# Self edges taken out of the gathers of a relational graph layer: compacted rows of 267 edges

## The chip, the cores and the metric

One core of a Trainium2 chip. The metric is the device time of one execution in microseconds, the median of several runs.

## The reference

A graph layer with a normalisation ahead of it and a residual sum behind it. 12500 nodes of 256 values, 212500 edges, 8 edge types. The edges are sorted by destination with a stable sort; 12500 of them go from a node to itself, and since they were appended last, each node's own edge is the last of its edges.

```python
def ref(edge_index, x, edge_type, weight, h_bias, loop_weight):
    src, dst = edge_index
    hx = einsum('ni,rio->rno', x, weight)            # one product per type
    msg = hx[edge_type, src]
    agg = segment_sum(msg, dst, num_segments=num_nodes)
    node_repr = agg * 0.5 ** 0.5 + h_bias
    return node_repr + (x @ loop_weight) * 0.5 ** 0.5

h = maximum(layernorm(x, axis=-1), 0.0)
return x + ref(stack([src, dst]), h, edge_type_8, weight, h_bias, loop_weight)
```

## The kernel before

The kernel sums first and multiplies afterwards: for every node and every type it adds up the rows of h whose edges arrive there, and only then applies the eight weights. Everything is fp32.

*Tiles and units.* 128 edges make a tile, two tiles a unit (`PAIR`): 1661 tiles, 831 units. The edge indices are loaded as rows of 256 (`load_indices`), one row per unit, 128 rows to a block, seven blocks. `sources` turns the source indices over, so that a column of `gidx` holds the 128 sources of a tile; `columns` works out for each edge a column, 8 times the node's distance from the row's first node plus the type, and `places` the row's offset in the accumulator.

*Edges.* `gather(t)` fetches the 128 rows of a tile from h by an indirect DMA on POOL (L479). `onehots` compares the columns with a constant row on VectorE (L492). `edge_sums` multiplies messages by one-hots on PE into PSUM (L520): 168 columns for a unit's first tile and 136 for its second (`REACH`), each in two chunks of 128 features. `add_sums` adds a unit's 336 columns into the accumulator at an offset held in a register (L532). Each fp32 matmul stands in the profile as two records.

*The accumulator.* `acc` is a ring of six slots (`SLOTS`), each of 128 nodes, features on partitions: `[128, 2, 8, 6 * 128 + 2 * WIN]`. A slot is zeroed on ScalarE by `clear` (L546), six groups ahead.

*Groups.* 98 groups of 128 nodes. When all units that can touch a group are added (`plan.last`), its work is queued: `own` transposes the group's rows of h into a PSUM buffer (tag `pt`, a pool of one buffer that all transposes use), copies them to `self_t`, and adds the bias to x; 18 products (L606: two with the loop weight, sixteen with the type weights) go into `po`; `finish` adds `po` to x, stores four groups at a time, and clears a slot. h and x come back from memory four groups at a time (`load_groups`, on SP's queue).

*The start.* h must exist before it is gathered. The kernel therefore reads all of x in pieces (`load_rows`), normalises on VectorE and ScalarE (`norm_rows`, `moments`) and stores h (`h32`). The first 96 tiles gather rows of x instead and are normalised in place (`batch`); later ones gather h.

*Order.* The order on each engine is written by hand: one loop over tiles, `gather` running 58 tiles ahead (`AHEAD`; 62 message buffers), one-hots 8 to 11 ahead (`LEAD`), `add_sums` one unit behind (`LAG`). Steps of the next block's preparation are put into a `background` list with the tile at which each is due. Group products are spread between edge sums by a budget: each has a cost and a tile by which it must be out (`until`).

```python
until = PAIR * (plan.first[g + SLOTS] - 2) - REST if g + SLOTS < plan.NG else NT - 1
ready = t + max(0, min(DELAY, NT - 1 - t - 2 * DELAY))
...
while queue and (budget > 0 and t >= queue[0][0] or t >= queue[0][1]):
```

*The fallback.* A count of edges that fitted their row's window is compared with the number of edges; if it differs, `general_path` computes everything anew, edge by edge.

Of the kernel before, what the change touches and what calls it, by code (L numbers as in the profile page):

```python
# [20 lines left out]
P = 128  # L21
# [4 lines left out]
XG = 4  # L26


WIN = 21
REACH = ((0, 21), (4, 17))  # L30
# [4 lines left out]
CLEARED = 3  # L35
# [23 lines left out]
PREP = 30  # L59
STEP = 3  # L60

# [3 lines left out]
class Plan:  # L65
# [6 lines left out]
    def __init__(self, N, E):  # L72
        self.NT = -(-E // P)
        self.NU = NU = -(-self.NT // PAIR)
        U = PAIR * P
        slack = 6.5 * (E / 4) ** 0.5 / U + 1.0
        self.rate = rate = E / (N * U)

        self.low = [(1 / rate, -slack / rate), (1.1 / rate, -(1.5 + 0.1 * E / U) / rate)]
        self.high = [(1 / rate, slack / rate)]  # L80
        self.starts = list(range(0, N, GROUP))
        self.ends = self.starts[1:] + [N]
        self.NG = len(self.starts)
        self.last = [
            min([NU - 1, *(int((e + 2 - b) / a) + 1 for a, b in self.low)]) for e in self.ends]
        self.last[-1] = NU - 1
        a, b = self.high[0]
        self.first = [max(0, int((s - WIN - 2 - b) / a) - 1) if s else 0 for s in self.starts]

# [101 lines left out]
def kernel(  # L191
# [20 lines left out]
    NJ = N // P  # L212
    NM = NJ * P
    NR = N - NM

    NT = plan.NT
    NTF = E // P
    EL = E - (NT - 1) * P

    U = PAIR * P  # L220
    NU = plan.NU
    NUF = E // U
    EU = E - NUF * U
    NB = -(-NU // P)
    scale = ALPHA**0.5
# [10 lines left out]
    zero = const.tile([P, 1], F32, name="zero")  # L236
    bias_in = const.tile([P, D], F32, name="bias_in")
    w = const.tile([P, KC, R * D], F32, name="w")
    wl = const.tile([P, KC, D], F32, name="wl")
    gidx = const.tile([P, NB * PAIR * P], I32, name="gidx")  # L240
    col = const.tile([P, NB, PAIR, P], F32, name="col")
    low = const.tile([P, NB], F32, name="low")
    high = const.tile([P, NB], F32, name="high")
    counts = const.tile([P, NB], F32, name="counts")
    flag = const.tile([1, 1], I32, name="flag")
    NK = -(-N // RING)
    wraps = const.tile([P, NK], F32, name="wraps")

    def edges(t):
        return P if t < NTF else EL  # L250
# [6 lines left out]
    with ExitStack() as main:  # L257
# [5 lines left out]
        rowp = main.enter_context(tc.tile_pool(name="rowp", bufs=ROWS))  # L263
        small = main.enter_context(tc.tile_pool(name="small", bufs=4))
        msgs = main.enter_context(tc.tile_pool(name="msgs", bufs=MSGS // PAIR))
        ohs = main.enter_context(tc.tile_pool(name="ohs", bufs=2 + LEAD // QUAD))
        dense = main.enter_context(tc.tile_pool(name="dense", bufs=2))
# [4 lines left out]
        iota_f, bias_bc = fixed[:, :C], fixed[:, C : C + D]  # L272
        assert C + D <= 512
# [3 lines left out]
        added, zeroed = {}, {}  # L277
# [3 lines left out]
        def load_indices(b):  # L281
            nat = {}
            for name, a, pad in (("s", src, 0), ("d", dst, -1), ("t", etype, 0)):
                n = ep.tile([P, U], I32, name=f"nat_{name}")
                full = min(P, NUF - b * P)
                if full < P:
                    nc.vector.memset(n, pad)
                e0 = b * P * U
                if full:
                    nc.sync.dma_start(  # L290
                        n[:full, :], a[e0 : e0 + full * U].rearrange("(p q) -> p q", q=U))
                if full < P and EU:
                    nc.sync.dma_start(
                        n[full : full + 1, :EU], a[NUF * U : E].rearrange("(p q) -> p q", p=1))
                nat[name] = n
            return nat

        def turned(got, cols, to):

            def turn():  # L300
                pt = ps_d.tile([P, D], F32, tag="pt", name="ptr")
# [3 lines left out]
                nc.vector.tensor_copy(to, pt[:, : PAIR * P])  # L305

            return [turn]

        def sources(b, got):
            def copy():  # L310
                got["sf"] = ep.tile([P, U], F32, tag="part", name="sf")
                nc.vector.tensor_copy(got["sf"], got["s"])

            return [copy] + turned(got, "sf", gidx[:, b * PAIR * P : (b + 1) * PAIR * P])

        def columns(b, got):
# [4 lines left out]
            def bases():  # L321
                got["base"] = small.tile([P, PAIR], F32, name="base")
                nc.vector.tensor_scalar(
                    got["base"][:, 0:1], got["d"][:, 0:1], low[:, b : b + 1], high[:, b : b + 1],
                    op0=ALU.max, op1=ALU.min)

            def second():
                nc.vector.tensor_scalar(
                    got["base"][:, 1:2], got["base"][:, 0:1], float(REACH[1][0]), None, op0=ALU.add)

            def relative():
                got["rel"] = ep.tile([P, U], F32, name="rel")
                for i, (h, _, _) in enumerate(halves):
                    nc.vector.tensor_scalar(
                        got["rel"][:, h], got["d"][:, h], got["base"][:, i : i + 1], None,
                        op0=ALU.subtract)

            def from_():
                got["ok"] = ep.tile([P, U], F32, tag="part", name="ok")
                nc.vector.tensor_scalar(got["ok"], got["rel"], 0.0, None, op0=ALU.is_ge)  # L340

            def to():
                for h, _, n in halves:
                    nc.vector.scalar_tensor_tensor(
                        got["ok"][:, h], got["rel"][:, h], float(n), got["ok"][:, h],
                        op0=ALU.is_lt, op1=ALU.mult)

            def typed():
                nc.vector.scalar_tensor_tensor(
                    got["rel"], got["rel"], float(R), got["t"], op0=ALU.mult, op1=ALU.add)  # L350

            def final():
                nc.vector.scalar_tensor_tensor(
                    got["rel"], got["rel"], 1.0, got["ok"], op0=ALU.add, op1=ALU.mult)
                nc.vector.tensor_reduce(counts[:, b : b + 1], got["ok"], AX.X, ALU.add)

            return [bases, second, relative, from_, to, typed, final] + turned(
                got, "rel", col[:, b, :, :].rearrange("p i u -> p (i u)"))

        def places(b, got):  # L360
# [16 lines left out]
            def turn():  # L377
                pt = ps_d.tile([P, D], F32, tag="pt", name="ptr")
# [6 lines left out]
        def verdict(got):  # L385
# [5 lines left out]
            def compare():  # L391
                pt = ps_d.tile([P, D], F32, tag="pt", name="ptr")
# [10 lines left out]
        def prepare(b):  # L403
# [3 lines left out]
                lambda: got.update(load_indices(b)), *sources(b, got), *columns(b, got),  # L407
                *places(b, got), *(verdict(got) if b == NB - 1 else [])]


        x_main = x[:NM].rearrange("(p j) d -> p j d", p=P)
        h_main = h32[:NM].rearrange("(p j) d -> p j d", p=P)
        groups = [(j, min(XG, NJ - j), P) for j in range(0, NJ, XG)]
        if NR:
            groups.insert(1, (NJ, 1, NR))

# [24 lines left out]
        def load_rows(i):  # L441
            if i < len(groups):
                j0, nj, n = groups[i]
                xts[i] = rowp.tile([P, XG, D], F32, tag="rows", name="xt")
                if n == P:
                    nc.sync.dma_start(xts[i][:, :nj, :], x_main[:, j0 : j0 + nj, :])
                else:
                    nc.sync.dma_start(xts[i][:n, 0, :], x[NM:])

        def norm_rows(i):  # L450
            j0, nj, n = groups[i]
            xt = xts.pop(i)
            after = moments([xt[:n, j, :] for j in range(nj)], n, nj, "n_")

            def rest():
                after()
                if n == P:
                    nc.sync.dma_start(h_main[:, j0 : j0 + nj, :], xt[:, :nj, :])
                else:
                    nc.sync.dma_start(h32[NM:], xt[:n, 0, :])  # L460
# [5 lines left out]
        def gather(t):  # L466
            n = edges(t)
# [6 lines left out]
            else:  # L474
# [3 lines left out]
            at = (b * PAIR + i) * P + u  # L478
            nc.gpsimd.indirect_dma_start(  # L479
                out=msg[t][:n], out_offset=None, in_=table[:, :],  # L480
                in_offset=bass.IndirectOffsetOnAxis(ap=gidx[:n, at : at + 1], axis=0))

        def onehots(t):
# [5 lines left out]
            for v, i in ((n // PAIR, PAIR), (1, n % PAIR)):  # L489
                if v and i:  # L490
                    cols = col[:, b, :i, u + k : u + k + v].rearrange("p i u -> p u i")
# [3 lines left out]
                        cols.unsqueeze(3).to_broadcast([P, v, i, C]), op=ALU.is_equal)  # L495
# [13 lines left out]
        def edge_sums(t):  # L509
            n = edges(t)  # L510
# [8 lines left out]
            for c in range(KC):  # L519
                nc.tensor.matmul(  # L520
                    ps[:, c, from_ : from_ + width], m[:n, c * P : (c + 1) * P], o[:n, :width],
# [6 lines left out]
        def add_sums(u, ps):  # L528
# [5 lines left out]
            for g in range(1, plan.NG):  # L534
                if plan.first[g] == u:
                    assert not plan.first[g] or (g, "slot") in zeroed
                    for k in [k for k in zeroed if k[0] == g or k[1] == "wrap"]:
                        tc.add_manual_dep(
                            i.ins, zeroed.pop(k).name, SYNC_DEP, reason="columns are empty")


        def clear(g):

            s0 = plan.starts[g] % RING
            a = acc[:, :, :, s0 : s0 + GROUP].rearrange("p c r d -> p (c r) d")
            i = nc.scalar.activation(a, zero.unsqueeze(2).to_broadcast([P, KC * R, GROUP]), AF.Copy)  # L546
            zeroed[g, "slot"] = i.ins
# [3 lines left out]
        def load_groups(q):  # L551

            d0, d1 = plan.starts[XG * q], plan.ends[min(plan.NG, XG * (q + 1)) - 1]
            full, rest = divmod(d1 - d0, P)
            for name, table in (("h", h32), ("x", x)):
                rows_ = got[name, q] = rowp.tile([P, XG, D], F32, tag="rows", name=f"{name}r")
                if full:
                    nc.sync.dma_start(
                        rows_[:, :full, :],
# [270 lines left out]
```

## Time and profile before

| | |
|---|---|
| median of 3 runs | 2112.68 us (2111.18 to 2114.15) |
| profiled execution | 2568.97 us, its span 2567.2 us |
| PE busy in the profile | 2019.2 us (79%), 10405 records |
| VectorE | 920.8 us (36%) |
| ScalarE | 342.8 us (13%) |
| POOL | 1572.7 us (61%) |
| granted TensorE clock, mean | 0.891 |
| gathers L479 | 1661, 946 ns each |
| edge sums L520 | 6644 records |
| products L606 | 3528 records |

The profiled execution is one execution with the profiler on, and its time is its own; the median is of executions without it. A row of a group ends with the busy time, the mean of one instruction in ns, and the idle time ahead of it with what ended it. "issue" is idle time for which the profile shows no cause. A timeline row starts with start and length in us. Ends of matmuls are modelled.

### The profile page before, as it was taken

How to read it: one execution, taken by the hardware profiler on the slowest of the kernel's cores; microseconds unless marked ns; L12 is line 12 of the kernel's file. 1: busy time of each engine (PE TensorE's matmuls, PEld its weight loads, DVE VectorE, ACT ScalarE, POOL GpSimd, SP SyncE). 2: the span in 40 equal slices, each digit the busy share in tenths (PEclk: the TensorE clock that was granted, in tenths of full speed). 3: DMA queues.
4: the chain of work that ended last, by engine and by line, in shares of the span. 5: the costliest groups of instructions: out<-in, count | busy, mean ns of one | idle time of the engine just before them, and what ended most of it. 6: DMA issues, size and time to landing. Idle time of an engine off the chain costs nothing.

```text
span 2567.2 us, 28487 instructions
## 1 busy us (share of the span) xinstructions
PE 2019.2 (79%) x10405; PEld 1736.7 (68%) x10405; DVE 920.8 (36%) x2101; ACT 342.8 (13%) x446; POOL 1572.7 (61%) x1686
## 2 busy tenths in 40 slices
PE   1148888888888788888888888888888888878789
PEld 1137767677777677677767676777667676667678
DVE  3476333333333333333333333333333333343333
ACT  3574101010100101011010100101001010101010
POOL 7435666666666666666666666666666666666640
PEclk9558899898898989889888999999898889999999
DMA  5682433333433333343333343333333333333320
GB/s 185 202 294 85 119 88 115 115 91 115 120 90 115 102 102 116 91 119 113 92 114 116 90 121 115 88 115 101 108 115 92 114 115 91 115 114 92 114 82 13
DMA packets 131293, 288.61 MB, mean 112 GB/s; under 512 B 29032, under 2 KB 71878, under 8 KB 131152
## 3 DMA queue, kind: packets, MB, share of 16 engines
q0 software_dynamic: 79712, 217.71, 29.2%
q1 hardware_dynamic: 51440, 69.05, 8.2%
q8 instruction: 85, 1.39, 0.2%
q14 instruction: 56, 0.46, 0.1%
HBM read 261.04 MB, written 25.60 MB: 112 GB/s over the span
## 4 chain that ended last, share of the span: by engine, by line
PE 75%; issue 17%; DVE 3%; another core or an unknown queue 2%; ACT 1%; DMA 1%; POOL 0%; SPq 0%; DVEq 0%; ACTq 0%; POOLq 0%
PE ps L520 40%; PE po L606 34%; PE pst L573 1%; DVE e_stats L422 1%; DMA h<-xt 1%; ACT xt L434 0%; DMA w<-in_L_gnn_weight_dram 0%; DVE n_stats L422 0%; ACT msg L434 0%; DVE n_mv L424 0%; DVE acc L532 0%; POOL msg L479 0%; DVE e_mv L424 0%; DVE oh L492 0%
## 5 line engine op out<-in xcount | busy, mean ns | idle before, releaser
L479 POOL DMA_INDIRECT msg<-h,gidx x1565 | 1480.2, 946 | 829.7 <-issue 417.0
L520 PE MATMUL ps<-oh,msg 128*128 128x168 f32 x6644 | 1301.7, 317 | 376.2 <-issue 230.1
L520 PEld LDWEIGHTS ps<-oh,msg 128*128 128x128 f32 x6644 | 1157.5, 208 | 563.3 <-issue 344.4
L606 PE MATMUL po<-w,acc 128*128 128x256 f32 x3136 | 1008.4, 410 | 114.0 <-issue 106.9
L606 PEld LDWEIGHTS po<-w,acc 128*128 128x128 f32 x3136 | 563.8, 206 | 181.4 <-issue 164.6
L532 DVE TENSOR_TENSOR acc<-acc,ps 128x336 f32 x831 | 413.7, 498 | 679.5 <-PE ps L520 350.9
L492 DVE TENSOR_TENSOR oh<-fixed,col 128x672 f32<-128x672 f32 x416 | 354.5, 852 | 770.9 <-remote 360.6
L546 ACT ACTIVATE acc<-zero 128x2048 f32<-128x2048 f32 x98 | 187.2, 1912 | 682.8 <-PE ps L520 374.5
L575 ACT ACTIVATE self_t<-pst 128x256 f32<-128x256 f32 x98 | 37.4, 382 | 1397.5 <-remote 650.4
L479 POOL DMA_INDIRECT msg<-in_x_dram,gidx x96 | 91.0, 947 | 82.9 <-issue 58.9
L606 PE MATMUL po<-wl,self_t 128*128 128x256 f32 x392 | 120.0, 418 | 24.6 <-issue 20.3
L606 PEld LDWEIGHTS po<-wl,self_t 128*128 128x128 f32 x392 | 73.1, 206 | 46.5 <-issue 38.4
L434 ACT ACTIVATE xt<-xt,n_shift,n_rstd 128x256 f32<-128x256 f32 (+1 forms) x98 | 50.9, 588 | 21.5 <-DVE n_shift L431 7.3
L434 ACT ACTIVATE msg<-msg,e_shift,e_rstd 128x256 f32<-128x256 f32 x96 | 49.8, 589 | 24.9 <-DVE e_shift L431 10.3
L573 PE MATMUL pst<-ident,hr 128*128 128x128 f32 x196 | 40.2, 285 | 15.9 <-issue 13.9
L615 DVE TENSOR_TENSOR xr<-xr,po 128x256 f32<-128x256 f32 x98 | 40.4, 413 | 10.7 <-PE po L606 7.8
L573 PEld LDWEIGHTS pst<-ident,hr 128*128 128x128 f32 x196 | 28.6, 149 | 20.4 <-issue 16.2
L576 DVE TENSOR_TENSOR xr<-xr,fixed 128x256 f32<-128x256 f32 x98 | 40.5, 413 | 3.6 <-issue 3.6
L422 DVE BATCH_NORM_STATS2 n_stats<-xt 128x6 f32<-128x256 f32 (+1 forms) x98 | 34.4, 412 | 0.8 <-issue 0.8
L422 DVE BATCH_NORM_STATS2 e_stats<-msg 128x6 f32<-128x256 f32 x96 | 33.5, 411 | 0.0
L424 DVE BATCH_NORM_AGGREGATE n_mv<-n_stats 128x2 f32<-128x6 f32 (+1 forms) x98 | 10.1, 156 | 15.7 <-issue 7.5
L430 DVE RECIPROCAL n_rstd<-n_rstd 128x4 f32<-128x4 f32 (+2 forms) x26 | 4.4, 170 | 26.9 <-issue 14.6
(61 smaller groups left out, 112.9 us busy)
## 6 DMA issues: line engine op xcount, KB each, us to landing
msg<-h,gidx POOLq DMA_INDIRECT x1565
xt<-in_x_dram SPq DMA_DIRECT2D x24, 512.0 KB
h<-xt SPq DMA_DIRECT2D x24, 512.0 KB
hr<-h SPq DMA_DIRECT2D x24, 512.0 KB
xr<-in_x_dram SPq DMA_DIRECT2D x24, 512.0 KB
out_dram<-xr SPq DMA_DIRECT2D x24, 512.0 KB
w<-in_L_gnn_weight_dram SPq DMA_DIRECT2D x2, 1024.0 KB
msg<-in_x_dram,gidx POOLq DMA_INDIRECT x96
```

Of the source, the lines that this page charges most:

```text
L422: nc.vector.bn_stats(stats[:n, j, :], rows_[j])
L434: nc.scalar.activation(rows_[j], rows_[j], AF.Relu, bias=shift[:n, j : j + 1], scale=rstd[:n, j : j + 1])
L479: nc.gpsimd.indirect_dma_start(out=msg[t][:n], out_offset=None, in_=table[:, :], in_offset=bass.IndirectOffsetOnAxis(ap=gidx[:n, at : at + ...
L492: nc.vector.tensor_tensor(o[:, k : k + v, :i, :], iota_f.unsqueeze(1).unsqueeze(1).to_broadcast([P, v, i, C]), cols.unsqueeze(3).to_broadc ...
L520: nc.tensor.matmul(ps[:, c, from_ : from_ + width], m[:n, c * P : (c + 1) * P], o[:n, :width], start=(i == 0 and c == 0), stop=(end and c ...
L532: i = nc.vector.tensor_tensor(a, a, ps, op=ALU.add)
L546: i = nc.scalar.activation(a, zero.unsqueeze(2).to_broadcast([P, KC * R, GROUP]), AF.Copy)
L573: nc.tensor.transpose(pst[:, c, :n], hr[:, c * P : (c + 1) * P], ident[:n, :n])
L575: nc.scalar.activation(got["self", g][:, :, :n], pst[:, :, :n], AF.Copy)
L576: nc.vector.tensor_add(xr, xr, bias_bc[:n])
L606: i = nc.tensor.matmul(got["out", g][:n], lhs, rhs, start=(r == R and c == 0), stop=(r == R - 1 and c == KC - 1))
L615: nc.vector.tensor_add(rows_[:n, k, :], rows_[:n, k, :], got["out", g][:n])
```

## The change

A row now holds 267 edges. The last edge of every node in it is taken out, if it is the node's own, and what is left fits 256 places. Per block, `sources` packs source, distance and type of every edge into one integer in PSUM (`packed`), and moves the kept ones to the left in five steps, each an AND and a predicated copy (`compacted`). `last_edges` does the same for the edges taken out, in nine steps, and leaves in `loops` the type of each node's own edge. There are 796 units and 1592 tiles. `WIN` is 22, so the two tiles of a unit have 176 and 144 columns.

The part of the own edges is written when a group's slot is begun (`begin`, in the place of `clear` and `own`): h of the group is transposed and copied to `self_t`, and eight VectorE operations write, for each type, the transposed rows where the node's own edge has that type and zero elsewhere. The types of 512 nodes, the same on all partitions, come from `find_types`: matmuls of 512 bf16 columns with one column of `loops` spread over the stationary operand, 22 for each block that can hold nodes of the four groups.

The bias is now a product with a row of ones at the head of the group's products. The first six groups are begun during the normalisation, whose pieces are now 512 consecutive nodes. Blocks are prepared 300 tiles ahead, three steps at one tile; `gidx` and `col` are buffers per block.

```diff
-WIN = 21
-REACH = ((0, 21), (4, 17))
+EDGES = 267
+WIN = 22
+REACH = ((0, 22), (4, 18))
...
-PREP = 30
+PREP = 300
 STEP = 3
+OPS = 3
...
+        def compacted(got, bit, bits):
+            def step(k):
+                m = work_tile(got, "moves", 6, I32)
+                nc.vector.tensor_single_scalar(m, packed, 1 << (bit + k), op=ALU.bitwise_and)
+                nc.vector.copy_predicated(
+                    packed[:, : EDGES - (1 << k)], m[:, 1 << k :], packed[:, 1 << k :])
+            return [lambda k=k: step(k) for k in range(bits)]
...
+            return [rises, stays, shifts, codes, packs, *compacted(got, TB, SB), unpacks,
+                    *turned(got, "sf", lambda: gidx.setdefault(b, idx.tile([P, U], I32, name="gidx")))]
...
+            return [selves_, ends, moves, codes, packs, number,
+                    *compacted(got, TB + 1, (EDGES - 1).bit_length()), kept]
...
             def rest():
                 after()
-                if n == P:
-                    nc.sync.dma_start(h_main[:, j0 : j0 + nj, :], xt[:, :nj, :])
-                else:
-                    nc.sync.dma_start(h32[NM:], xt[:n, 0, :])
+                nc.sync.dma_start(rows_of(h32, i), xt[:n, :k, :])
+                for g in range(d // P, min(d // P + k, SLOTS, plan.NG)):
+                    begin(g, xt[:, g - d // P, :])
                 load_rows(i + ROWS - 2)
...
-        def clear(g):
-            s0 = plan.starts[g] % RING
-            a = acc[:, :, :, s0 : s0 + GROUP].rearrange("p c r d -> p (c r) d")
-            i = nc.scalar.activation(a, zero.unsqueeze(2).to_broadcast([P, KC * R, GROUP]), AF.Copy)
+        def begin(g, rows_):
+            n = plan.ends[g] - plan.starts[g]
+            pst = ps_d.tile([P, 512], F32, tag="pt", name="pst")
+            pst = pst[:, : KC * P].rearrange("p (c d) -> p c d", c=KC)
+            for c in range(KC):
+                nc.tensor.transpose(
+                    pst[:, c, :n], rows_[:n, c * P : (c + 1) * P], ident[:n, :n])
+            got["self", g] = selves.tile([P, KC, GROUP], F32, name="self_t")
+            copy = nc.scalar.activation(got["self", g][:, :, :n], pst[:, :, :n], AF.Copy)
+            q, k = divmod(g, XG)
+            of = typed[q][:, k * GROUP : k * GROUP + n].unsqueeze(1).to_broadcast([P, KC, n])
+            s0 = g % SLOTS * GROUP
+            for r in range(R):
+                i = nc.vector.scalar_tensor_tensor(
+                    acc[:, :, r, s0 : s0 + n], of, float(r + 1), pst[:, :, :n],
+                    op0=ALU.is_equal, op1=ALU.mult)
+                if r == 0:
+                    tc.add_manual_dep(i.ins, copy.ins.name, SYNC_DEP, reason="one reader at a time")
+
+        def find_types(q):
...
+            pt = ps_d.tile([P, 512], F32, tag="pt", name="ptt")
+            for b in bs:
+                o = types.tile([P, XG * GROUP + WIN - 1], BF16, name="places")
+                nc.vector.tensor_scalar(
+                    o, line, firsts[b], float(WIN - 1 - d0), op0=ALU.subtract, op1=ALU.is_equal)
+                for k in range(WIN):
+                    nc.tensor.matmul(
+                        pt[:, :n], loops[b][:, k : k + 1].to_broadcast([P, P]),
+                        o[:, WIN - 1 - k : WIN - 1 - k + n],
+                        start=(b == bs[0] and k == 0), stop=(b == bs[-1] and k == WIN - 1))
+            typed[q] = types.tile([P, XG * GROUP], BF16, name="types")
+            nc.scalar.activation(typed[q][:, :n], pt[:, :n], AF.Copy)
...
                 if (r, c) == (R, 0):
                     got["out", g] = ps_o.tile([P, D], F32, name="po")
+                    nc.tensor.matmul(
+                        got["out", g][:n], one[:, :n], bias_in, start=True, stop=False)
...
-                if g + SLOTS < plan.NG:
-                    clear(g + SLOTS)
+                b = g + SLOTS
+                if b < plan.NG:
+                    begin(b, got["h", b // XG][:, b % XG, :])
+                if b % XG == XG - 1:
+                    find_types(b // XG + 1)
+                if b % XG == XG // 4 and b // XG >= 2:
+                    load_groups("h", h32, b // XG + 1)
```

## The prediction

> **What bounds the kernel now.** I read the page first: which engine is busiest, what the chain is made of, what one instruction costs.
>
> ```profile
> PE 2019.2 (79%) x10405; PEld 1736.7 (68%) x10405; DVE 920.8 (36%) x2101; ACT 342.8 (13%) x446; POOL 1572.7 (61%) x1686
> ...
> PE 75%; issue 17%; DVE 3%; another core or an unknown queue 2%; ACT 1%; DMA 1%; POOL 0%; SPq 0%; DVEq 0%; ACTq 0%; POOLq 0%
> ...
> L479 POOL DMA_INDIRECT msg<-h,gidx x1565 | 1480.2, 946 | 829.7 <-issue 417.0
> L520 PE MATMUL ps<-oh,msg 128*128 128x168 f32 x6644 | 1301.7, 317 | 376.2 <-issue 230.1
> ```
>
> TensorE looks like the bound: 75% of the chain. But this page is of an execution of 2568.97 us (span 2567.2), 456 us above the median of 2112.68, so part of it is not in the timed runs. The candidate is "issue": 17% of the chain, 436 us in which PE waited for nothing shown. Windows say when it happens (columns: PE, PEld, DVE, ACT, POOL busy, clock, DMA share, GB/s):
>
> ```profile
> 140.00:160.00 20.00, 7.52 (x25) 6.62 (x26) 16.86 (x78) 16.24 (x37) 7.55 (x8) 0.50 0.92 332
> ...
> 2380.00:2480.00 100.00, 81.39 (x433) 70.32 (x431) 33.84 (x63) 9.35 (x9) 65.88 (x70) 0.93 0.36 107
> 2490.00:2560.00 70.00, 68.98 (x410) 62.67 (x409) 25.58 (x51) 1.84 (x5) 0.00 (x0) 1.00 0.03 11
> ```
>
> While POOL gathers, PE is 81% busy; once gathers are over, 99%. The gathers themselves, in the timeline, where nothing holds them:
>
> ```profile
> 7.49 0.95 POOL L479 DMA_INDIRECT msg<-in_x_dram,gidx  x1 [0.30 <-issue]
> 8.75 0.95 POOL L479 DMA_INDIRECT msg<-in_x_dram,gidx  x1 [0.31 <-issue]
> 10.00 0.95 POOL L479 DMA_INDIRECT msg<-in_x_dram,gidx  x1 [0.30 <-issue]
> ```
>
> One each 1.25 us, instruction 0.95 and gap 0.30. 1661 x 1.25 = 2076; with the first at 4.8, the last ends at 2081. Behind it come two last groups, 36 products x 0.431 = 15.5, and a store: about 2101. That is within 12 us of the median. Now PE without stalls, from the chain of waits in order of time:
>
> ```profile
> 906.80 0.46 PE ps L520 x4
> 907.26 0.43 PE po L606 x2
> 907.69 0.57 PE ps L520 x4
> 908.26 0.86 PE po L606 x4
> ```
>
> An fp32 matmul is two records: a first-half tile (168 columns) 0.57, a second-half one (136) 0.46 (0.462 unrounded), a product (256) 0.43 per two records: 0.844 ns per column and record, no gaps between kinds. So PE needs 831 x 0.57 + 830 x 0.462 = 857, plus 1764 products x 0.431 = 760, transposes 43, others 6: 1666 us. I read the timed runs as POOL-bound (1.25 per tile against PE's 1.0), with some 300 us of slack on PE, and the profiled execution as PE-bound through stalls that the profiling adds.
>
> **The change part by part.** *Gathers.* 267 edges per row instead of 256 give 796 units, 1592 tiles: 69 gathers fewer, 69 x 1.25 = -86 us on POOL.
>
> *PE.* Edges: 176 and 144 columns, 0.597 + 0.489 per unit, x796 = 864 (+7). A bias product per group, 98 x 0.431 = +42. Transposes: same number. New: the type of each node's last edge is spread over the partitions by 22 matmuls of 512 bf16 columns per (four groups, block), 34 such sets, 748 matmuls. No row here is bf16. The nearest is fp32, 0.844 x 512 = 0.432 us per record: 318 us in all. The Trainium skill (TensorE: Matmul & The Clock Gate, "Wait — 56ns, not 53.3ns?") puts a warm matmul at columns / 2.4 GHz + 2.5 ns, 0.2157 for 512; a record of 256 fp32 columns here takes 0.215, two such steps per column, so fp32 passes are what doubles it. I take the page's: 159 us (upper end 318). PE: 1666 + 7 + 42 + 159 = 1874.
>
> *A new wait on PE.* All transposes and the type matmuls share one PSUM buffer, `pt`. After every fourth `begin`, `find_types` stands right behind its transposes in PE's queue, so PE, and behind it all edge sums and products, waits for: ScalarE's copy (0.38, row self_t 383 ns), eight VectorE operations of 256 elements from PSUM (row xr<-xr,po: 413 ns, 3.3), `places` of 533 elements (about 0.6), and signals: 4.9 us, 23 times after the start: 113. From below: nothing if VectorE ran ahead, which the buffer excludes; from above, slow signals, in rival C. Index preparation puts three operations into one tile's slot, its transposes waiting for VectorE, some 20 us. The clock: windows of 100 us here grant 0.88 to 0.95 with PE idle 17%. The same page has an idle window of 3.4 us halving the clock; by it half of 23 waits cost a 3.4 us window at half speed, 20 us; a granted mean of 0.95 over all of PE's work would cost 5% of 1839, 92. I take 20, since PE is now nearly always busy.
>
> *The start.* Norms run on VectorE and ScalarE, both over 80% busy at 140:160; x gathers (96) last until they end. With the stalls of 20 to 90 us left out, I put that end at 112 us before. What now comes ahead of it: 19 operations before the first gather (0.46 start to start, as L349 to L353): first gather at 13.6 instead of 4.8. Then 26 more for the last edges (11 us) and 20 for columns, `find_types` twice (6.5 cold, 4.8), and six `begin`s in series on `pt`, 4.4 each (transposes 0.5, copy 0.4, eight operations 3.3, signals 0.2) = 26. Step by step the statistics of the fourth row piece move from 18.5 to about 86 us. Then part of block 1's preparation (30 operations, 12 us, mostly beside waits), and rows in 1 KB pieces: the trace's DMA records have 46 ns for 1 KB, 159 for 4 KB, +16%, at most 10 us. Norms end at about 190 (from 165 if half of it overlaps).
>
> *Costed at nothing.* VectorE gains 784 x 0.413 = 325 and index work of about 25 instead of 5 us in each of 7 blocks, loses 41 (bias adds) and 32: some 1340 of 2100 us. Four PSUM banks and one-hots eight tiles ahead cover its 4 us bursts; without that cover each of 98 would cost PE up to 2. ScalarE loses 98 clears, 187 us, off the path. SP: the 24 h loads become 23 and are issued two to three groups earlier; in SP's queue only other loads and stores stand behind them, none due within 60 us. POOL gets one iota more (0.3). The Trainium skill (SBUF — State Buffer, "Who interferes with whom") lets a one-source fp32 VectorE operation lock GpSimd out: some 80 such new ones x 0.36 = 30 us by the rule. In the trace gathers beside such index work are 940/946/1277 ns (min/median/max): I take 0, 30 in the range.
>
> *Sum, timed runs.* PE after the start: edges of 1562 tiles 848, products and bias 802, transposes 40, types (32 sets) 149 = 1839. 190 + 1839 + waits 153 + ramp until the weights are scaled 10 + store 5 = 2197; I say 2190. POOL: h gathers from about 195, 1496 x 1.25 = 1870, tail 25: 2090. PE is the later. *Profiled execution:* 2569 + 208 work + 23 waits of about 9 (three signals of some microseconds) + start 70 + stalls for 7% more records 31: about 3085.
>
> **The rivals.** A is the forecast: PE takes over, 2110 to 2280.
>
> B, POOL remains the bound. For it: 69 gathers are the only work on the present bound, and PE's 1874 is below POOL's 1990. It decides if norms end before about 150 and waits stay near 60: 150 + 1839 + 60 + 15 = 2064, and POOL 155 + 1870 + 25 = 2050; with no delay at all 13.6 + 1990 + 25 = 2029. Against it: PE has only 1.16 of 1.25 us per tile left for everything. Faster: 2030 to 2108.
>
> C, slow signals and stalls are not only the profiler's.
>
> ```profile
> 1004.05 0.38 PE L573 MATMUL pst<-ident,hr 128*128 128x128 f32 x2
> ...
> 1006.21 0.38 ACT L575 ACTIVATE self_t<-pst 128x256 f32<-128x256 f32 x1 [14.38 <-PE ps L520]
> ...
> 2492.34 0.38 PE L573 MATMUL pst<-ident,hr 128*128 128x128 f32 x2
> ...
> 2492.82 0.38 ACT L575 ACTIVATE self_t<-pst 128x256 f32<-128x256 f32 x1 [8.45 <-PE pst L573]
> ```
>
> With gathers running the copy starts 1.8 us behind its transposes (median over all groups 4.2), without them 0.1. Before, PE's slack hid this in timed runs. The new wait has three such hops: 23 x 3 x 2 to 4 = 140 to 290 more: 2330 to 2480. Against it: the median leaves the start no such delay.
>
> That the change doesn't do its work: if a row of 267 edges held under 11 last edges, or a last edge were no self edge, the whole fallback would run, in milliseconds; a row has 15.7 on average, and the reference sorts the self edge last. 0.01.
>
> **How the numbers follow.** A 0.54, B 0.22, C and the fallback 0.21, no change 0.03: within 0.2%, about what a measurement of this kernel can tell from none, is 2108.5 to 2116.9, a thin slice between A and B. Time 2190 (A's own range 2110 to 2280). The range takes most of B, without its bottom, and of C up to 2390: 2055 to 2390.
>
> **What would show it.** Right: L701 records near 216 ns, PE gaps ended by VectorE before every fourth group's types, norms ending some 70 us later, PE busier in a steady 100 us than 83, POOL waiting more for PE. Wrong: POOL gathers at 1.25 us throughout with PE waiting for messages (B); waits above 10 us at L701 (C); bf16 records of 0.43.

## The result and the profile after

| kernel | median, us | ratio to before, 95% interval |
|---|---|---|
| before | 2113.41 (2111.18 to 2114.31) | |
| changed | 2236.46 (2231.84 to 2238.67) | 1.0583 [1.0568, 1.0598] |

The change costs 123 us, 5.8%. The forecast was 2190 in a range of 2055 to 2390, with slower at 0.75.

The runs fell on chips of two speeds. On one chip, the slow chip below, the kernel before takes 2568.55 us in plain timed runs (2566.83 to 2571.01, 7 runs), on the others, called the usual chip, about 2112. The profile shown before the prediction (2568.97 us) fits the slow chip; the result above and all experiments but the first four are from the usual one. Whether it is the chip, or something about it at that time, is not known: its timed runs are all of one occasion.

The page of the changed kernel, in its rows for engines, for the chain that ended last, and for the groups that answer to those shown of before:

```profile
PE 1984.4 (89%) x11073; PEld 1699.8 (76%) x11073; DVE 1290.3 (58%) x3124; ACT 170.4 (8%) x373; POOL 1512.0 (68%) x1618
...
PE 78%; DVE 13%; issue 3%; ACT 2%; POOL 1%; DMA 1%; DVEq 0%; SPq 0%; ACTq 0%; POOLq 0%
...
L607 POOL DMA_INDIRECT msg<-h,gidx x1496 | 1417.4, 947 | 544.8 <-issue 405.9
L647 PE MATMUL ps<-oh,msg 128*128 128x176 f32 (+1 forms) x6368 | 1103.7, 305 | 79.9 <-ACT msg L567 51.7
...
L679 DVE SCALAR_TENSOR_TENSOR acc<-types,pst 128x256 f32<-128x256 bf16 (+1 forms) x784 | 267.5, 413 | 113.7 <-ACT self_t L674 113.7
L701 PE MATMUL ptt<-places,loops 128*128 128x512 bf16 (+1 forms) x748 | 210.7, 452 | 95.6 <-DVE places L698 94.9
```

The fair partner is not the page shown first but a page of the unchanged kernel on the usual chip (`before_again` below; span 2110.4):

```profile
PE 53%; DMA 25%; issue 10%; POOL 7%; DVE 2%; ACT 2%; SPq 0%; DVEq 0%; ACTq 0%; POOLq 0%
...
L479 POOL DMA_INDIRECT msg<-h,gidx x1565 | 1480.5, 946 | 481.3 <-issue 346.1
L520 PE MATMUL ps<-oh,msg 128*128 128x168 f32 x6644 | 1204.7, 308 | 262.1 <-DMA msg<-h,gidx 153.5
```

Read the two chains against each other. Before, a third of the chain is gathers (DMA 25%, POOL 7%), and what PE waits for is messages. After, the chain is 78% PE and POOL 1%. Behind 205 us, POOL's gaps above its usual 0.30 sum to 83 us after the change and to 0.1 before it. The windows of the steady part say it once more (columns: PE, PEld, DVE, ACT, POOL busy, clock, DMA share, GB/s). Unchanged kernel, usual chip:

```profile
700.00:800.00 100.00, 88.80 (x500) 71.42 (x500) 38.62 (x71) 10.63 (x10) 75.63 (x81) 1.00 0.41 121
900.00:1000.00 100.00, 88.26 (x500) 75.04 (x499) 40.52 (x78) 11.48 (x10) 75.63 (x81) 0.97 0.41 122
```

Changed kernel:

```profile
700.00:800.00 100.00, 94.45 (x538) 80.59 (x537) 61.53 (x135) 2.52 (x6) 72.11 (x76) 0.98 0.41 120
900.00:1000.00 100.00, 96.09 (x551) 83.97 (x550) 54.04 (x110) 2.52 (x6) 74.22 (x80) 0.97 0.41 120
```

75.63 of POOL in 100 us is the ceiling, a gather every 1.25 us (0.95 and a gap of 0.30). The unchanged kernel sits on it in every window taken between 200 and 2000 us. The changed one is below it in nine of the ten windows taken between 300 and 2100 us (66 to 74; the tenth has 75.64), with PE at 92 to 96 in all but one. The lead of the gathers settles it: counted in the traces at five times between 500 and 1900 us, 2 to 7 more tiles are gathered than summed before the change, and 52 to 58 after it, where the program allows 58. The bound has moved from POOL to PE.

**The start.** The last normalised piece, in the timeline of ScalarE, changed kernel and then the unchanged one:

```profile
186.17 0.60 ACT L567 ACTIVATE xt<-xt,n_shift,n_rstd 84x256 f32<-84x256 f32 x1 [0.42 <-DVE n_shift L564]
```

```profile
109.34 0.60 ACT L434 ACTIVATE xt<-xt,n_shift,n_rstd 128x256 f32<-128x256 f32 x1 [0.43 <-DVE n_shift L431]
```

77 us later. The first product follows at 203.5 instead of 134.1.

**The wait at the types.** PE, ScalarE and VectorE in the timeline of the changed kernel, around one `find_types`:

```profile
240.98 0.38 PE L671 MATMUL pst<-ident,hr 128*128 128x128 f32 x2
247.57 7.81 PE L701 MATMUL ptt<-places,loops 128*128 128x512 bf16 x22 [6.21 <-DVE places L698]
...
243.95 0.36 ACT L674 ACTIVATE self_t<-pst 128x256 f32<-128x256 f32 x1
...
244.34 2.74 DVE L679 SCALAR_TENSOR_TENSOR acc<-types,pst 128x256 f32<-128x256 bf16 x8 [1.28 <-ACT self_t L674]
247.00 0.51 DVE L698 TENSOR_SCALAR places<-line,firsts 128x533 bf16<-128x533 f32 x1
```

Between the transposes and the type products PE does nothing, while ScalarE copies (here late, as it was still normalising messages) and VectorE writes eight parts and `places`. In the steady part the same gap is 3.7 to 3.9 us; all 23 behind the start sum to 94 us of idle PE. And it has a tail. The windows around it (PE busy second column, granted clock third from the end):

```profile
238.50:241.50 3.00, 2.86 (x21) 2.57 (x19) 3.00 (x11) 2.19 (x5) 2.39 (x3) 1.00 0.41 112
241.50:247.50 6.00, 0.00 (x0) 0.00 (x0) 4.67 (x15) 2.37 (x6) 4.48 (x6) 0.93 0.35 102
247.50:249.50 2.00, 1.93 (x5) 0.73 (x6) 2.00 (x11) 0.00 (x0) 1.42 (x2) 0.50 0.44 123
249.50:251.50 2.00, 2.00 (x6) 0.71 (x5) 0.44 (x2) 0.00 (x0) 0.94 (x1) 0.50 0.41 111
251.50:253.50 2.00, 2.00 (x7) 0.64 (x6) 0.00 (x0) 0.00 (x0) 0.00 (x0) 0.51 0.07 25
253.50:255.30 1.80, 1.80 (x9) 0.67 (x7) 0.00 (x0) 0.00 (x0) 0.00 (x0) 1.00 0.00 0
```

The clock is at 0.50 as the type products begin and back at 1.00 six microseconds later. Measured from one start to the next, a type record of 512 columns takes 217 ns (median), and some 200 of the 704 behind the start take about 427; those cost 42 us. Not every wait has the tail. The trace's record of the clock has a stretch at 0.50 behind 21 of the 23 waits; behind two of them, at 1682 and 1948 us, it has none. Here 44 records follow a wait of 3.72 us and take 0.22 each:

```profile
1682.24 9.69 PE L701 MATMUL ptt<-places,loops 128*128 128x512 bf16 x44 [3.72 <-DVE places L698]
```

### The profile page after: what moved, and what is told of

It reads as the page before. It is cut to its first block, busy times and chain, and to the rows that moved or that the text cites. A ratio compares the mean times of both kernels' runs of the same rounds, so it can differ in the third digit from the quotient of the medians.

```text
span 2236.7 us, 30467 instructions
## 1 busy us (share of the span) xinstructions
PE 1984.4 (89%) x11073; PEld 1699.8 (76%) x11073; DVE 1290.3 (58%) x3124; ACT 170.4 (8%) x373; POOL 1512.0 (68%) x1618
## 4 chain that ended last, share of the span: by engine, by line
PE 78%; DVE 13%; issue 3%; ACT 2%; POOL 1%; DMA 1%; DVEq 0%; SPq 0%; ACTq 0%; POOLq 0%
PE ps L647 34%; PE po L758 31%; PE ptt L701 9%; DVE acc L679 4%; PE po L752 2%; DVE oh L620 1%; POOL msg L607 1%; DVE acc L659 1%; DVE moves L331 1%; PE pst L671 1%; DVE fixed L332 1%; DVE e_stats L555 1%; DVE n_stats L555 1%; ACT xt L567 1%; ACT self_t L674 0%
## 5 line engine op out<-in xcount | busy, mean ns | idle before, releaser
L607 POOL DMA_INDIRECT msg<-h,gidx x1496 | 1417.4, 947 | 544.8 <-issue 405.9
L647 PE MATMUL ps<-oh,msg 128*128 128x176 f32 (+1 forms) x6368 | 1103.7, 305 | 79.9 <-ACT msg L567 51.7
L647 PEld LDWEIGHTS ps<-oh,msg 128*128 128x128 f32 x6368 | 1028.6, 194 | 154.3 <-ACT msg L567 54.8
L758 PE MATMUL po<-w,acc 128*128 128x256 f32 x3136 | 870.2, 380 | 0.8 <-DVE flag L521 0.8
L620 DVE TENSOR_TENSOR oh<-fixed,cols 128x704 f32<-128x704 f32 x398 | 353.3, 888 | 445.4 <-PE ps L647 439.9
L659 DVE TENSOR_TENSOR acc<-acc,ps 128x352 f32 x796 | 409.3, 514 | 285.4 <-PE ps L647 278.9
L679 DVE SCALAR_TENSOR_TENSOR acc<-types,pst 128x256 f32<-128x256 bf16 (+1 forms) x784 | 267.5, 413 | 113.7 <-ACT self_t L674 113.7
L701 PE MATMUL ptt<-places,loops 128*128 128x512 bf16 (+1 forms) x748 | 210.7, 452 | 95.6 <-DVE places L698 94.9
L701 PEld LDWEIGHTS <-loops 128*128 128x128 bf16 x748 | 83.3, 114 | 217.2 <-DVE places L698 99.1
L752 PE MATMUL po<-bias_in,one 1*128 1x256 f32 x196 | 68.6, 429 | 0.9 <-DVE xr L767 0.9
```

The source lines that it names most:

```text
L607: nc.gpsimd.indirect_dma_start(out=msg[t], out_offset=None, in_=table[:, :], in_offset=bass.IndirectOffsetOnAxis(ap=gidx[b][:, at : at + 1 ...
L620: nc.vector.tensor_tensor(o[:, k : k + v, :i, :], iota_f.unsqueeze(1).unsqueeze(1).to_broadcast([P, v, i, C]), of.unsqueeze(3).to_broadcas ...
L647: nc.tensor.matmul(ps[:, c, from_ : from_ + width], m[:, c * P : (c + 1) * P], o[:, :width], start=(i == 0 and c == 0), stop=(end and c == ...
L659: i = nc.vector.tensor_tensor(a, a, ps, op=ALU.add)
L679: i = nc.vector.scalar_tensor_tensor(acc[:, :, r, s0 : s0 + n], of, float(r + 1), pst[:, :, :n], op0=ALU.is_equal, op1=ALU.mult)
L701: nc.tensor.matmul(pt[:, :n], loops[b][:, k : k + 1].to_broadcast([P, P]), o[:, WIN - 1 - k : WIN - 1 - k + n], start=(b == bs[0] and k == ...
```

## The experiments

Four kernels ran on the slow chip, eight on the usual one. Each ratio is to the kernel before on the same chip.

**Fewer gathers, on the slow chip.** `b_fewer` is the kernel before with 65 gathers left out, `a_fewer` the changed one with 62:

```diff
 def gather(t):
...
+    if t > 96 and t % 24 == 23:
+        msg[t] = msg[t - 1]
+        return
```

> The kernel before, with 65 of its 1661 gathers left out (every 24th tile from 119 on uses the message of the tile in front of it); all matmuls, additions and one-hots stay, so those 65 tiles add the wrong rows. If the timed runs of before are bound by POOL's gathers at 1.25 us, the time falls by 65 x 1.25 = 81 us, to about 2032. If PE (or its stalls) is the bound, it stays within 10 us of 2113.

Measured: 2480.44 us against 2568.55, ratio 0.9653 [0.9636, 0.9669], so 88 us for 65 gathers, 1.355 each. The time follows the gathers on this chip, but not because POOL runs them back to back. The largest of TensorE's waits in its trace (total, times, longest), and one window:

```profile
PE ps L523 <- issue: 208.2, 351, 1.7
```

```profile
700.00:800.00 100.00, 86.77 (x453) 74.89 (x452) 38.39 (x82) 9.99 (x9) 65.08 (x69) 0.90 0.36 106
```

POOL is at 65, not at 75.6, and PE still stalls for no shown cause. What the stalls are is not settled, and one reason is that these traces cannot tell. The pages of the slow chip, the one shown before the prediction among them, give no time from issue to landing for the gathers (first line; the second is the usual chip):

```profile
msg<-h,gidx POOLq DMA_INDIRECT x1565
msg<-h,gidx POOLq DMA_INDIRECT x1565, 2.8
```

With no landing on record, a wait of PE for a message cannot be named, and can stand there as "issue".

> The changed kernel with 62 of its 1592 gathers left out in the same way, all else kept. If PE is the bound now, nothing: 2236 within 5 us. If POOL still sets the end (late start, then 1.25 us a tile), 62 x 1.25 = 77 us less: 2159.

Measured: 2700.67 us, 1.0522 [1.0477, 1.0567] of the kernel before. Inconclusive: the changed kernel itself was not run on that chip, so there is nothing to subtract from. The same holds for the next two on that chip; they came again on the usual one. Neither kernel with fewer gathers was run on the usual chip: that POOL sets the time there before the change, and not after it, rests on the windows and leads above and on the experiments below.

**The order of types and slot, and the bias.** In `a_first` (and again `a_first2`) `find_types` comes ahead of `begin` in a group's `finish`, so that PE is not made to stand behind the slot's eight VectorE operations:

```diff
+    if b % XG == XG - 1:
+        find_types(b // XG + 1)
     if b < plan.NG:
         begin(b, got["h", b // XG][:, b % XG, :])
-    if b % XG == XG - 1:
-        find_types(b // XG + 1)
```

In `a_bias` (and again `a_bias2`) the bias is added on VectorE, and its products are taken off PE (the load of the bias onto all partitions is left out here):

```diff
-nc.tensor.matmul(got["out", g][:n], one[:, :n], bias_in, start=True, stop=False)
...
 nc.vector.tensor_add(rows_[:n, k, :], rows_[:n, k, :], got["out", g][:n])
+nc.vector.tensor_add(rows_[:n, k, :], rows_[:n, k, :], bias_in[:n])
```

> The changed kernel with find_types called before begin instead of behind it, so that its matmuls wait for the operation places alone and not for eight operations and a copy of begin. If the wait of PE on the one transpose buffer costs what the trace shows (3.9 us 23 times = 90, and some 45 us of matmuls at half clock behind it), begin then waits about 1 us for ScalarE's copy of the types and the time falls by 90 to 110 us, to about 2135. If the wait is only passed on to begin's transposes, or POOL takes over at once, it falls by less than 30.

> The changed kernel with the bias added on VectorE again (98 additions of 0.41 us in finish) and the 98 bias products taken out of PE. PE-bound, at what the trace of after shows from start to start (0.31 us for each of two records): 98 x 0.62 = 61 less, 2175. At the prediction's price for it (0.431): 42 less, 2194. If PE is not the bound: 2236.

On the slow chip: 2692.66 us, 1.0489 [1.0461, 1.0518], and 2774.02 us, 1.0802 [1.0784, 1.082]. Without the changed kernel beside them only their order can be read: there, taking away the wait leaves less than taking away the bias.

**The changed kernel, half the type products, later preparation, and four edits together**, on the usual chip. The changed kernel again:

> The changed kernel, unchanged, timed beside the kernel before on the chip that the next three share. If the price of the change is the same on every chip (work on TensorE and waits of fixed length), it is 1.058 of the kernel before here too, or 2.236 ms where that takes 2.113. If cross-engine signals and TensorE stalls differ between chips, then on a chip where the kernel before takes 2.57 ms the changed one takes about 2.75 to 2.85 ms (1.07 to 1.11).

2237.3 us, 1.059 [1.0572, 1.0607]: the same price on another usual chip. `a_half` makes 11 of the 22 type products of a set:

```diff
-for k in range(WIN):
+for k in range(0, WIN, 2):
```

> Only every second of the 22 type products of a set is made (half of the types are left out): 374 matmuls of 512 bf16 columns fewer on TensorE, the eviction, the copies and the wait for VectorE stay. Theory TensorE-bound: 374 x 0.217 = 81 us, minus the 18 us of the start's and the part that half-speed records after the wait add back (45 us excess over all 748, half of it more): 75 to 105 us less than the changed kernel. Rival, GpSimd's gathers bound it: under 15 us less.

Measured: 2170.84 us, 66 below the changed kernel and short of the 75 to 105 expected. In the traces, the type records behind the start take 83 us less from start to start: 352 x 0.217 = 76, and 7 of half-speed records. The half-speed loss fell only from 44 to 37 us with half of the records, so it belongs to the wait and not to what follows. The first product came 7 us earlier, as the start has type products too. Some 22 us were lost again in one gap of TensorE: its "issue" waits before edge sums are 28.2 us against 10.0, 22.4 of it in that gap, which ends at 1707 us and whose cause `a_first2` shows below. POOL's column is back at its ceiling; the gathers are still 43 to 60 tiles ahead of the sums, so PE doesn't wait for them:

```profile
900.00:1000.00 100.00, 96.19 (x558) 84.87 (x558) 54.16 (x111) 2.51 (x6) 75.69 (x80) 0.98 0.41 121
1100.00:1200.00 100.00, 95.62 (x560) 85.52 (x559) 57.15 (x118) 2.51 (x6) 75.71 (x80) 0.98 0.42 126
```

`a_prep` begins a block's preparation later:

```diff
-PREP = 300
+PREP = 200
```

> Preparation of a block's indices starts 200 tiles ahead instead of 300, so that block 1's 60 VectorE operations fall behind the norms instead of among them (tile 56 instead of 0). Theory that VectorE's extra work delays the start: the norms end 12 to 20 us earlier and the whole is 10 to 20 us shorter than the changed kernel. Rival, the start is held by the rows' and gathers' transfers: within 5 us. If the later preparation comes too late for the gathers (58 tiles ahead) it would be longer by tens of us.

Measured: 2233.53 us, 4 less. The number is the one expected of the rival (within 5 us), but its reason is not: the start did move. The first step was right: the last normalised piece is at 165.3 instead of 186.2, and the first product at 182.5 instead of 203.5. But the 21 us came back later: PE's idle gaps behind 205 us sum to 129 us against 113, the waits for VectorE at the types and at the index transposes being longer. VectorE's preparation has to be done at some place, and PE waits for it there.

`a_best` has four edits: `find_types` first, bias on VectorE, preparation 200 tiles ahead, and the last block's padding made by one iota at the start and copied by VectorE when it is needed.

> Four edits together: find_types ahead of begin in a finish, the bias added on VectorE instead of by 98 matmuls, the last block's iota made once at the start and copied by VectorE, preparation 200 tiles ahead. TensorE theory on a chip where the changed kernel takes 2236: 75 (wait behind pst) + 60 (bias) + 25 (late iota) + 12 (start) = 170 less, but the gathers end at about 2085, so 2085 to 2110: level with or 1% below the kernel before. On a chip where the kernel before takes 2.57 ms: 2.60 to 2.65 ms. If the bias and the wait are hidden anyway: within 30 us of the changed kernel.

Measured: 2105.91 us (2103.6 to 2107.64), 0.9973 [0.9962, 0.9983] of the kernel before: 131 us below the changed kernel and 5.5 below the old one, so level with it within 0.3%. It is at POOL's ceiling in most steady windows, and the gathers' lead shrinks from 48 tiles at 500 us to 5 at 1900:

```profile
700.00:800.00 100.00, 97.81 (x577) 84.72 (x575) 56.43 (x116) 2.29 (x6) 75.62 (x81) 1.00 0.41 122
900.00:1000.00 100.00, 98.31 (x589) 87.70 (x588) 59.08 (x127) 2.90 (x7) 75.63 (x81) 1.00 0.42 124
```

And its last gather, in POOL's timeline, starts 24 us before the end:

```profile
2080.68 0.94 POOL L607 DMA_INDIRECT msg<-h,gidx  x1 [0.30 <-issue]
```

**The unchanged kernel's profile, and the order alone, on the usual chip.**

> The kernel before, unchanged, profiled on another chip than the page shown first. If its profile was long only because the profiler added stalls, the span is near 2567 us again and the timed runs beside it 2112. If the chip makes the difference, then on a chip whose timed runs take 2112 the span is about 2110 too, gathers start 1.25 us apart throughout (79 or 80 in 100 us), TensorE shows no 'issue' stalls in its waits and waits for messages instead, and the norms end some 70 us earlier than in the changed kernel (112 against 187 us). On a chip whose timed runs take 2569 the page of before comes back.

Measured: 2111.95 us, span 2110.4. The profiler adds nothing to speak of; the difference lies between the chips. The second alternative holds, with the gathers on their ceiling and PE's largest wait for messages, as shown above.

> The changed kernel with find_types ahead of begin in a finish, so that TensorE does not stand behind begin's eight VectorE operations. On a chip where the changed kernel takes 2237 us: the wait theory says 23 x 3.9 = 90 us less of the wait behind pst, and up to 45 us less of half-speed records behind it, minus some new waits of the transposes for the types' copy (23 x 0.6 = 14): 75 to 120 us less, 2117 to 2162 (1.003 to 1.024 of the kernel before); the gathers' own end at about 2090 does not hold it yet. If the wait only moves to another place: 2215 to 2240. On a chip where the kernel before takes 2569 us: 1.049 of it, as measured.

Measured: 2165.32 us, 1.0247 [1.023, 1.0264]: 72 less, just short of the 75 to 120 expected. TensorE's waits behind `places`, in the changed kernel and in this one (total, times, longest):

```profile
PE ptt L701 <- DVE places L698: 94.9, 24, 8.5
```

```profile
PE ps L647 <- issue: 38.3, 6, 30.6
...
PE ptt L701 <- DVE places L698: 17.1, 13, 6.9
PE pst L671 <- ACT types L706: 15.6, 23, 0.7
```

78 us of waits are gone, and 16 came in their place as expected. The loss by half-speed records fell from 42 to some 5 us (22 type records are missing from this trace, and the doubled steps that they leave are not counted). That makes 99, and the first row takes 28 of it back: "issue" was 10.0 in the changed kernel, and is 38.3 here, 30.6 of it in one gap. PE's timeline names no cause; VectorE's and POOL's at that time do:

```profile
1711.27 3.87 PE L647 MATMUL ps<-oh,msg 128*128 128x176 f32 x16 [30.64 <-issue]
...
1672.38 0.28 DVE L302 MEMSET nat_t<- 128x267 int32 x1
1709.11 0.44 DVE L341 TENSOR_TENSOR rise<-nat_d 128x267 f32<-128x267 int32 x1 [36.44 <-DMA nat_d<-in_dst_dram]
...
1705.86 0.95 POOL L607 DMA_INDIRECT msg<-h,gidx  x1 [0.30 <-issue]
1706.83 0.37 POOL L299 IOTA nat_d<- 128x268 int32 x1
```

The last block's preparation starts with an iota on POOL. It stands in POOL's queue behind the gathers that the program puts ahead of it, and 27 of them start between VectorE's last operation and the iota; the load of `nat_d` waits for the iota, `rise` on VectorE waits for the load, and the one-hots and sums that PE needs stand behind `rise`. POOL was not busy with anything long: it had a queue of 1.25 us gathers. In the changed kernel the same place cost less, VectorE 10.0 us (longest wait at `rise`), since POOL was further ahead of PE there: 54 tiles at 1650 us, against 35 in `a_first2`, so that only 6 gathers were left to start ahead of the iota. The faster PE is, the more this place costs: a gap of 4.2 us behind 6 gathers in the changed kernel, 22.4 behind 20 in `a_half`, 30.6 behind 27 here.

**The iota alone, and the bias alone.** `a_first_iota` is `a_first2` with that iota made once at the start:

```diff
+nc.gpsimd.iota(rising, pattern=[[2, EDGES + 1]], base=N - 2 * EU, channel_multiplier=0)
 load = prepare(0)
...
-nc.gpsimd.iota(n, pattern=[[2, EDGES + 1]], base=N - 2 * EU, channel_multiplier=0)
+nc.vector.tensor_copy(n, rising)
```

> find_types ahead of begin, and the last block's iota made once at the start and copied by VectorE, so that no VectorE operation waits for GpSimd in the middle. With find_types ahead alone it was 2165 us, and its trace has TensorE idle for 30.6 us at 1680 us while VectorE waits 36.4 us for nat_d behind an iota that stands behind 24 gathers. If that is the whole story: 25 to 32 us less, 2133 to 2140 us on a chip where the kernel before takes 2112 (1.010 to 1.013 of it). If the gathers that POOL is then ahead by would have been lost anyway (gathers bind): within 10 us of 2165. On a chip where the kernel before takes 2569 us, where GpSimd runs no gathers ahead: under 10 us less than 1.049 of it.

Measured: 2132.57 us, 1.0098 [1.0081, 1.0115]: 33 less than `a_first2`, where 25 to 32 were expected. The longest wait of `rise` is now

```profile
DVE rise L341 <- DMA nat_d<-in_dst_dram: 11.8, 3, 6.9
```

> The changed kernel with the bias added on VectorE after the sum with x, and the 98 bias products off TensorE; everything else as it is. On a chip where the changed kernel takes 2237 us: the bias products' 196 records take 61 us from start to start, which are 61 us less if TensorE bounds it throughout: 2170 to 2185 (1.028 to 1.035 of the kernel before). By the prediction's 42 us: 2195. If VectorE's 98 further operations (41 us) delay buffers: above 2200. On a chip where the kernel before takes 2569 us: 1.080 of it, as measured.

Measured: 2182.19 us, 1.0331 [1.0313, 1.0348]: 55 less than the changed kernel, more than the prediction's 42 and less than 61. The rows of the changed kernel show that a bias product is dearer than its columns:

```profile
1744.37 0.69 PE L752 MATMUL po<-bias_in,one 1*128 1x256 f32 x2
1745.00 1.13 PE L758 MATMUL po<-wl,self_t 128*128 128x256 f32 x4
1745.96 0.76 PE L647 MATMUL ps<-oh,msg 128*128 128x176 f32 x4
```

Its two records take 0.63 from start to start, not 0.43, and the four of the next products 0.96 instead of 0.86: with them the bias costs 0.73 per group, 72 us in all. Why one partition costs more is not shown. The iota's place took part of that back, as in `a_first2`: a gap of 15.5 us, where the changed kernel has 4.2.

## Why the prediction was right, and where not

*The bound before.* Right for the timed runs: POOL at 1.25 us per gather, 2101 by the sum against 2112, and PE behind it with slack. The reason given for the page shown was wrong: "the profiled execution as PE-bound through stalls that the profiling adds". Profiled on the usual chip the kernel takes 2110.4, and on the slow chip it takes 2569 without a profile; and the "issue" that was read as stalls can be waits for messages, as that trace has no landings. So the expected 3085 for the changed kernel's profile fell with it (2236.7), and what is shown of rival C's slow signals belongs to that chip: on the usual one the copy starts 0.1 us behind its transposes (median over all groups, with gathers running, in both kernels).

*The start.* Norms at about 190 from 112: 186 from 109. First product 203.5 against 200. The parts of that sum were not tested one by one; `a_prep` shows that block 1's preparation was 21 us of it, not 12.

*PE's work.* Measured from start to start behind 203.5: edge sums 856 us (848 forecast), of which 11 are idle; types 197, which is 152 without half-speed records and other excess (149 forecast; the fp32 price would have been 318). The Trainium skill's 215.7 ns for 512 warm bf16 columns (TensorE: Matmul & The Clock Gate, "Wait — 56ns, not 53.3ns?") is 217 here. Products and bias 847 (802 forecast): this term failed. The 98 bias products were taken at their columns, 42; they cost about 72.

*The wait.* 113 forecast, 94 measured (mostly 3.7 us each instead of 4.9; the eight VectorE operations took 2.74 together, not 3.3). The clock behind it was the other failing term: 20 forecast on the ground that only half of the waits would halve it, 45 measured as excess over the median of the type records. The Trainium skill (TensorE: Matmul & The Clock Gate, "What's actually happening") has the clock at half after at least one idle window of about 3.4 us; one such window at half speed for each of the 23 waits gives 23 x 1.7 = 39 as an estimate, and was nearer than my half of it. The trace has the stretch behind 21 of the 23, of 3.4 or 6.8 us where nothing else adds to it.

*Costed at nothing.* "POOL gets one iota more (0.3)" named the iota's length and not its place in POOL's queue. In the changed kernel VectorE waits 10.0 us for it and PE loses 4.2 and then 8.5 at the next types; in `a_first2` the place costs 33. VectorE's total (1290 against 1340) and ScalarE's and SP's did not show on the path.

*The sum.* 190 + 10 to the first product, 1992 behind it and 5 for the store was 2197; measured 203.5, 2029 and 4. The 37 us behind the first product: products +45, types with their clock +28 (197 against 149 + 20), edge sums +8, transposes with the wait -24 (129 against 40 + 113), and -20 for index waits, which were put down on their own and are in the other terms when measured. With the two failing terms put right, 30 us of bias and 25 of clock, the sum would have been 2252, some 15 too high: the wait was taken 19 too long, and the 20 of index waits lie in the other terms. That the sum came within 40 us is in part luck, since errors of both signs met; that PE would bound the kernel, and through which wait, is not. *Rival B* failed as described: it needed norms before 150 and waits near 60. The forecast's own number for POOL, 2090 with 25 us behind the last gather, is what `a_best` came near once PE was relieved: 2105.91, with 24 behind it.

*Where the expected gain went.* 69 gathers at 1.25 are 86 us of POOL, and they were freed. They are worth nothing while PE, with some 230 us of new work (7 edges, 72 bias, 152 types) and 140 of waits and slow clock behind a start 77 us later, ends after POOL.

## What to carry to other kernels

Work taken from the busiest engine pays only up to the next one's total, and that total must hold the waits that the new work makes on it and the slow clock behind each. Where one in-order engine needs a result of another, ask what stands ahead of the producer in its own queue at that moment: a 0.37 us iota behind 27 gathers cost 33 us, and making it at the start took them back. Where one buffer serves two uses, issue first the one whose reader frees it soonest: with the types first, PE waits for one copy (0.7 us) instead of a copy, eight operations and `places` (3.7), and swapping two statements was worth 72 us here. And before reading "issue" as a stall, see whether the page gives the DMAs' times to landing.

## What the runs showed of the hardware

- Two chips, one kernel: 2112 against 2569 us in timed runs. On the slow one, in `b_fewer`, PE has 351 waits without a shown cause before edge sums (0.6 us on average, up to 1.7; landings are not on record), and ScalarE's copy starts 4.0 us behind PE's transposes (median) instead of 0.1.
- A bf16 record of 512 columns took 217 ns at full clock and 427 at half. Waits of the same 3.72 us were followed by a half-speed stretch of 3.4 us, of 6.8, or by none (1682 and 1948 us); 23 waits cost 45 us so, some 2 each.
- A product over one partition (1x256 fp32) took 304 to 320 ns per record from start to start, where one over 128 partitions took 216, and the record behind it took 320 too.
- With VectorE busy for 58 to 63% of the span instead of 44%, index operations included, the gathers on POOL took 947 to 950 ns each (946 before).
